# Masked attention on compacted slots: the context's products of two slot blocks run in a row, with nine buffers for exponentials instead of five

## The chip, the cores and the metric

The kernel runs on one core of one Trainium2 chip, as one launch. The metric is the device time of that launch in microseconds; the figure for the kernel before is the median of three runs. Traces come from one further execution that the hardware profiler recorded.

The engines are named as the profile names them: PE is the matrix engine, PEld its weight loads, ACT the engine of the exponentials and of most copies out of PSUM, DVE the vector engine, POOL the engine that issues indirect gathers and scatters, SP the queue that issues all other DMAs.

## The reference, cut to what matters

```python
x = x + _L0_cond_ref(x, cond_2048, L0_cond_Wq, L0_cond_Wo)   # x: 16 x 512 x 1024

B, D, T = x.shape                     # 16, 512, 1024; NH = 8 heads of dk = 64
scale = 1.0 / jnp.sqrt(dk)
xt = jnp.transpose(x, (0, 2, 1))
q = xt @ Wq.T
qh = q.reshape(B, T, NH, dk).transpose(0, 2, 1, 3)
scores = scale * jnp.einsum('bhqd,bhkd->bhqk', qh, qh)
cmask = mask[:, None, None, :]
rmask = mask[:, None, :, None]
logits = (scores * cmask + (1.0 - cmask) * NEG) * rmask
attn = jax.nn.softmax(logits, axis=-1)
ctx = jnp.einsum('bhqk,bhkd->bhqd', attn, qh)
ctx = ctx.transpose(0, 2, 1, 3).reshape(B, T, D)
out = ctx @ Wo.T
return jnp.transpose(out, (0, 2, 1))
```

The mask is 0 or 1, about half of each. Query, key and value are the same tensor. A masked key gets no weight, and a masked query gets the plain mean over all tokens.

## The kernel before, in words

**Compaction.** Per batch only the unmasked tokens take part in the attention. They are gathered (POOL, indirect DMA) into C = 544 slots: four blocks of 128 and a tail of 32. Masked tokens get one projected mean row per batch. A check at the end falls back to a plain version when a batch does not fit; this does not happen here.

**Work per batch** (16 batches, `run`, lines 724 to 912). For each of the four pairs of heads p and each slot block i from 0 to 3, `scores` (line 497) is called once for each of the two heads. It makes four f16 products on PE (line 530: 128 x 128 weights, 272 columns; a high and a low half of q, two column halves) into one of two PSUM buffers `pss`, and ACT writes the exponentials (line 533) into a tile `p` of 128 x 544 f32, from a ring of five. The scores are symmetric, so the tile serves directly as the right operand of the context.

`attend(b, p, i, ps)` (line 538) multiplies the two heads' exponentials of block i by the values: four f32 products (line 546: 128 x 64 weights, 272 columns), two for the upper and two for the lower half of the 128 output rows, summed over i in the one PSUM tile `pav`. The profile counts each of these f32 products as two records, so one block is eight records of L546. `attend(b, p, 4, None)` adds the tail (line 549, four records) and ACT copies `pav` to a tile `c` (line 553). Since there is one `pav`, the first product of the next pair waits for this copy.

The tail's own scores, `scores(b, k, None)`, come twice per batch, once for heads 0 to 3 and once for heads 4 to 7: 16 small products (line 510), an exponential (line 513) into the same ring, a split on DVE (lines 518, 519), and four SP DMAs (lines 523, 524) that fill the one tile `pt` which line 549 reads for two pairs. `recip` (line 557) makes the reciprocal sums and has them broadcast by DMA into `rb`; `norm` (line 590) multiplies `c` by `rb` on DVE and splits it for the output projection.

**What sets the order.** A batch has 18 places in a list `S`: the 16 pairs (p, i), and two places for the tails' scores, inserted at places 2 and 11. At each place `run` first calls what is due in `free` (loads, `recip`, `norm`), then the scores of the two heads, then `fill`, then `now`. `fill` is a share of other work `m`, dealt out by hand-written costs in proportion to the place: of the batch after, the transposes of x (line 358), the query products (line 380, cost 1.37 per call of 12 products) and the value transposes (line 423); of the batch before, the output projection (line 625, cost 2.6 per call of 12 products). In the second half of the places a large fill goes ahead of `now`. For a middle batch the costs dealt to places 0 to 17 are 1.45, 2.17, 1.37, 0.55, 1.37, 2.6, 1.37, 0, 2.6, 0.5, 2.6, 0.7, 1.37, 2.74, 0.55, 1.47, 2.6, 0.7.

`now` holds `attend` of the place before: each block's context runs one place after its scores. `attend(b, p, 4)` of pair p goes between the two heads' scores of block 1 of pair p + 1 (the lists `whole` and `tail`); for the last pair it follows block 3's in the next batch's first place.

The calls' order is a priority, not yet the order on an engine: when the program is built, a scheduler takes for each engine the first instruction that it thinks ready, and the engine then executes that fixed order.

Of the kernel before, what the change touches and what calls it, by code (L numbers as in the profile page):

```python
# [10 lines left out]
F32 = mybir.dt.float32  # L11
# [8 lines left out]
P = 128  # L20
# [10 lines left out]
C = 544  # L31
# [18 lines left out]
class Fast:  # L50
# [446 lines left out]
    def scores(self, b, p, i):  # L497


        nc, s = self.nc, self.st[b]  # L500
        if "z" not in s:
            s["z"] = self.sb([P, H, 4], F32, "z", 2)
            s["zt"] = self.sb([P, 2], F32, "zt", 2)
        if i is None:
            pt = self.ps_s.tile([P, 2, 512], F32, tag="s", name="pss")
            for a in range(2):
                for g in range(2):
                    for r in range(HG):
                        xx, k = s["xx"][2 * p + r // 2], r % 2
                        nc.tensor.matmul(pt[r * CT:(r + 1) * CT, g, :CH], lhsT=xx[:, 2 * k, 512:C],  # L510
                                         rhs=xx[:, 2 * k + a, g * CH:(g + 1) * CH], start=(a == 0), stop=(a == 1))
            t = self.sb([P, C], F32, "p", 5)
            nc.scalar.activation(t.rearrange("p (g c) -> p g c", g=2), pt[:, :, :CH], AF.Exp,  # L513
                                 bias=s["nm"][p][:, HG:], scale=SCALE, accum_out=s["zt"][:, p:p + 1])

            hi = self.sb([P, C], F32R, "c", 3)
            lo = t.bitcast(F32R)
            nc.vector.tensor_copy(hi, t)
            nc.vector.tensor_tensor(lo, t, hi.bitcast(F32), ALU.subtract)
            s["pt"] = self.sb([P, 2, C], F32R, "pt")  # L520
            half = slice(0, DK), slice(DK, P)
            for k in range(2):
                nc.sync.dma_start(out=s["pt"][half[k], k, :].bitcast(F32), in_=hi[half[k]].bitcast(F32))
                nc.sync.dma_start(out=s["pt"][half[1 - k], k, :].bitcast(F32), in_=lo[half[k]].bitcast(F32))
            return None
        xx, k = s["xx"][p // 2], p % 2
        pt = self.ps_s.tile([P, 2, 512], F32, tag="s", name="pss")
        for a in range(2):
            for g in range(2):
                nc.tensor.matmul(pt[:, g, :CH], lhsT=xx[:, 2 * k, i * P:(i + 1) * P],  # L530
                                 rhs=xx[:, 2 * k + a, g * CH:(g + 1) * CH], start=(a == 0), stop=(a == 1))
        t = self.sb([P, C], F32, "p", 5)
        self.exp = [nc.scalar.activation(t.rearrange("p (g c) -> p g c", g=2), pt[:, :, :CH], AF.Exp,  # L533
                                         bias=s["nm"][p // HG][:, p % HG:p % HG + 1], scale=SCALE,
                                         accum_out=s["z"][:, p, i:i + 1]).ins]
        return t
# [187 lines left out]
    def run(self, flag):  # L724
        B = self.B
        L = lambda f, *a: lambda: f(*a)
        S = [(p, i) for p in range(NP) for i in range(4)]
        S.insert(2, (0, None))
        S.insert(11, (1, None))
        N = len(S)  # L730

        def xt(n):
# [68 lines left out]
        begin += [(0, L(self.load, "o", c)) for c in range(DC)]  # L801
        begin += [(0, L(self.range_x, 0, c)) for c in range(DC)] + [(0, L(self.range_w, "q"))]
        groups = [(g, min(h, B)) for g, h in ((2, 4), (4, 8), (8, 12), (12, 16)) if g < B]
        todo, whole, tail = [], [], []
        for b in range(B + 1):
            o, n = b - 1, b + 1
            if b == B:
# [2 lines left out]
            free, early, late = {}, [], []  # L810
# [67 lines left out]
            for st, (p, i) in enumerate(S):  # L878
                for f in free.get(st, []):
                    f()  # L880
                if i is None:
                    self.scores(b, p, None)
                else:
                    ps = [self.scores(b, 2 * p, i)]
                    if tail:
                        tail.pop()()
                    ps.append(self.scores(b, 2 * p + 1, i))
                goal = total * (st + 1) / N
                fill = []
                while pos < len(m) and (done + m[pos][0] / 2 <= goal or st == N - 1):  # L890
                    fill.append(m[pos])
                    done += m[pos][0]
                    pos += 1

                big = st >= 4 and [c >= 1 for c, _ in fill if c > 0.1][:1] == [True]
                fill = [f for _, f in fill]
                now = [] if i is None else todo
                for f in fill + now if big else now + fill:
                    f()
                if i is not None:  # L900
                    todo = [L(self.attend, b, p, i, ps)]
                if whole and i == 0:
                    tail.append(whole.pop())
                if i == 3:
                    (whole if p < 3 else todo).append(L(self.attend, b, p, 4, None))
                    if p < 3:
                        free.setdefault(st + 2, []).append(L(self.recip, b, p))
                        free.setdefault(st + 4, []).append(L(self.norm, b, p))
            self.st.pop(b - 4, None)
        bad = self.const.tile([1, 1], F32, name="bad")  # L910
        self.nc.vector.tensor_reduce(bad, self.ok[0:1, :], AX.X, ALU.add)
# [145 lines left out]
```

## Time and profile before

| | us |
|---|---|
| median of 3 runs (1238.45 to 1245.84) | 1238.76 |
| the profiled execution's own time | 1251.64 |
| its span, first to last instruction | 1249.9 |
| PE busy | 1140.9 |
| DVE busy | 714.8 |
| ACT busy | 693.6 |
| POOL busy | 296.0 |

The mean granted clock of PE in the profiled execution is 0.966. Busy time of PE counts pipelined products with modelled ends, so that the rows of a timeline overlap: what one product costs is read from start to start, not from its duration. In the lists of waits, a row names the waiting engine, its output tile and line, the engine and line that ended the wait, and then the total, the number of times and the longest.

### The profile page before, as it was taken

How to read it: one execution, taken by the hardware profiler on the slowest of the kernel's cores; microseconds unless marked ns; L12 is line 12 of the kernel's file. 1: busy time of each engine (PE TensorE's matmuls, PEld its weight loads, DVE VectorE, ACT ScalarE, POOL GpSimd, SP SyncE). 2: the span in 40 equal slices, each digit the busy share in tenths (PEclk: the TensorE clock that was granted, in tenths of full speed). 3: DMA queues.
4: the chain of work that ended last, by engine and by line, in shares of the span. 5: the costliest groups of instructions: out<-in, count | busy, mean ns of one | idle time of the engine just before them, and what ended most of it. 6: DMA issues, size and time to landing. Idle time of an engine off the chain costs nothing. (4 is left out here: it accounts for less than half of the span.)

```text
span 1249.9 us, 23817 instructions
## 1 busy us (share of the span) xinstructions
PE 1140.9 (91%) x8354; PEld 694.5 (56%) x8354; DVE 714.8 (57%) x2262; ACT 693.6 (55%) x1828; POOL 296.0 (24%) x299
## 2 busy tenths in 40 slices
PE   7889989998998999999898999999989989998787
PEld 6456555555665555556565555555556555655343
DVE  6576556484645648465464746647565564746433
ACT  5757555565665555556564656556456455545341
POOL 3010221222012123221124314121331222122631
PEclk8899999999999999989999999899999989999889
DMA  6645445555345555545456455454645545444631
GB/s 210 166 125 147 141 128 153 157 161 161 89 138 141 167 149 150 159 122 146 134 140 205 133 149 160 126 150 129 205 129 153 140 142 138 110 138 119 211 114 68
DMA packets 106479, 181.36 MB, mean 145 GB/s; under 512 B 28096, under 2 KB 46176, under 8 KB 106352
## 3 DMA queue, kind: packets, MB, share of 16 engines
q1 hardware_dynamic: 85168, 111.59, 33.4%
q0 software_dynamic: 21184, 68.18, 17.1%
q8 instruction: 68, 1.11, 0.4%
q14 instruction: 59, 0.48, 0.1%
HBM read 92.34 MB, written 33.87 MB: 101 GB/s over the span
## 5 line engine op out<-in xcount | busy, mean ns | idle before, releaser
L533 ACT ACTIVATE p<-pss,nm 128x544 f32<-128x544 f32 x512 | 363.8, 714 | 270.2 <-PE pss L530 190.1
L530 PE MATMUL pss<-xx 128*128 128x272 f16 x2048 | 309.7, 284 | 43.9 <-ACT p L533 24.5
L546 PE MATMUL pav<-p,v 128*64 128x272 f32 x2048 | 328.7, 411 | 15.3 <-issue 11.4
L530 PEld LDWEIGHTS <-xx 128*128 128x128 f16 x2048 | 186.1, 99 | 138.6 <-issue 106.2
L694 POOL DMA_INDIRECT y_out<-xa,idx x72 | 76.9, 1068 | 661.0 <-DVE xa L630 633.7
L546 PEld LDWEIGHTS pav<-p,v 128*64 128x64 f32 x2048 | 132.1, 137 | 134.5 <-issue 80.9
L380 PE MATMUL pm<-xh,wqh 128*128 128x274 f16 (+1 forms) x512 | 147.7, 288 | 20.0 <-ACT q L383 19.7
L380 PE MATMUL pm<-xh,wql 128*128 128x274 f16 (+1 forms) x512 | 147.4, 288 | 0.0
L380 PE MATMUL pm<-xl,wqh 128*128 128x274 f16 (+1 forms) x512 | 147.2, 287 | 0.0
L380 PEld LDWEIGHTS <-wqh 128*128 128x128 f16 x1024 | 101.6, 100 | 48.3 <-issue 25.9
L383 ACT ACTIVATE q<-pm 128x272 f32<-128x272 f32 (+1 forms) x128 | 50.9, 398 | 96.8 <-PE pm L380 69.6
L533 ACT ACTIVATION_READ_ACCUMULATOR p<-pss,nm 128x1 f32 x512 | 102.1, 199 | 0.0
L284 POOL DMA_INDIRECT xa<-x_in,idx x72 | 73.1, 1016 | 90.7 <-ACT p L513 52.1
L630 DVE SCALAR_TENSOR_TENSOR xa<-pm,xa 128x512 f32<-128x512 f32 (+1 forms) x61 | 42.1, 689 | 90.5 <-PE pm L625 86.7
L625 PE MATMUL pm<-woh,ch 128*128 128x512 f16 x240 | 92.8, 387 | 0.0
L625 PE MATMUL pm<-wol,ch 128*128 128x512 f16 x240 | 92.4, 385 | 0.0
L625 PE MATMUL pm<-woh,cl 128*128 128x512 f16 x240 | 92.1, 384 | 0.0
L309 ACT ACTIVATE xm<-xm 128x512 f32<-128x512 f32 x116 | 73.0, 630 | 1.6 <-DMA xm<-x_nat_in 1.6
L694 POOL DMA_INDIRECT y_out<-xi,idx x56 | 58.9, 1051 | 62.1 <-DVE r L568 21.7
L625 PEld LDWEIGHTS <-ch 128*128 128x128 f16 x480 | 47.5, 100 | 46.8 <-issue 3.5
L609 DVE TENSOR_TENSOR c<-c,rb 128x544 f32<-128x544 f32 x64 | 46.1, 721 | 43.7 <-DMA rb<-rd 38.6
L319 DVE SCALAR_TENSOR_TENSOR xl<-pm,xh 128x512 f16<-128x512 f32 (+1 forms) x75 | 44.3, 607 | 33.8 <-ACT xh L318 29.3
(194 smaller groups left out, 1550.6 us busy)
## 6 DMA issues: line engine op xcount, KB each, us to landing
xm<-x_nat_in SPq DMA_DIRECT2D x116, 256.0 KB
xx<-hl SPq DMA_DIRECT2D x256, 68.0 KB
xx<-hl SPq DMA_DIRECT2D x128, 136.0 KB
rb<-rd SPq DMA_DIRECT2D x128, 128.0 KB
pt<-c SPq DMA_DIRECT2D x64, 136.0 KB
pt<-p SPq DMA_DIRECT2D x64, 136.0 KB
ub<-ud SPq DMA_DIRECT2D x16, 256.0 KB
xi<-x_nat_in SPq DMA_DIRECT2D x8, 256.0 KB
```

Source lines behind the costliest of these rows:

```text
L284: self.pool = [self.nc.gpsimd.indirect_dma_start(out=tile[:n], out_offset=None, in_=self.x, in_offset=bass.IndirectOffsetOnAxis(ap=idx, ax ...
L309: self.nc.scalar.activation(s["xm"][k], s["xm"][k], AF.Copy, accum_out=s["ms2"][:, k:k + 1])
L319: self.xs = nc.vector.scalar_tensor_tensor(self.xl[dst], src, SX, self.xh[dst], ALU.mult, ALU.subtract).ins
L380: nc.tensor.matmul(pq, lhsT=w[:, c, e * P:(e + 1) * P], rhs=xx[:, c, cols], start=(k == 0), stop=(k == 3 * DC - 1))
L383: nc.scalar.activation(s["q"][:, e, cols], pq, AF.Copy, scale=1.0 / (SX * SW))
L530: nc.tensor.matmul(pt[:, g, :CH], lhsT=xx[:, 2 * k, i * P:(i + 1) * P], rhs=xx[:, 2 * k + a, g * CH:(g + 1) * CH], start=(a == 0), stop=(a ...
L533: self.exp = [nc.scalar.activation(t.rearrange("p (g c) -> p g c", g=2), pt[:, :, :CH], AF.Exp, bias=s["nm"][p // HG][:, p % HG:p % HG + 1 ...
L546: nc.tensor.matmul(s["pav"][k * DK:(k + 1) * DK, g, :CH], lhsT=s["v"][p][:, i, k * DK:(k + 1) * DK], rhs=ps[k][:, cols], start=(i == 0), s ...
L609: nc.vector.tensor_tensor(c, c, s["rb"][p], ALU.mult)
L625: nc.tensor.matmul(po[:cols.stop - cols.start], lhsT=a[:, e, cols], rhs=w[:, e, :], start=(e == 0 and k == 0), stop=(e == DC - 1 and k == 2))
L630: self.nc.vector.scalar_tensor_tensor(x, po, 1.0 / (SX * SW), x, ALU.mult, ALU.add)
L694: i = self.nc.gpsimd.indirect_dma_start(out=self.out, out_offset=bass.IndirectOffsetOnAxis(ap=idx, axis=0), in_=x, in_offset=None).ins
```

## The change

Five edits, all in the order of the work:

- The ring `p` has nine tiles instead of five, in both places where it is allocated.
- A block's `attend` is kept in `todo`. At blocks 0 and 2 of a pair, what stands in `todo` becomes `ready` and nothing of it runs; at blocks 1 and 3 what is `ready` runs as `now`. So blocks 0 and 1 run together at block 3, and blocks 2 and 3 together at block 1 of the next pair (with the tail's product behind them for the last pair of a batch, at the next batch's place 1).
- `attend(b, p, 4)` of pairs 0 to 2 moves from between the scores of the next pair's block 1 to between those of its block 2.
- The second tail's scores move from place 11 to place 13, behind blocks 2 and 3 of pair 2.
- `norm` of pairs 0 to 2 is due five places after block 3 instead of four.

```diff
-            t = self.sb([P, C], F32, "p", 5)
+            t = self.sb([P, C], F32, "p", 9)
...
-        t = self.sb([P, C], F32, "p", 5)
+        t = self.sb([P, C], F32, "p", 9)
...
-        S.insert(11, (1, None))
+        S.insert(13, (1, None))
...
-        todo, whole, tail = [], [], []
+        todo, ready, whole = [], [], []
...
                     ps = [self.scores(b, 2 * p, i)]
-                    if tail:
-                        tail.pop()()
+                    if i == 2 and whole:
+                        whole.pop()()
                     ps.append(self.scores(b, 2 * p + 1, i))
...
-                now = [] if i is None else todo
+
+                now = []
+                if i in (0, 2):
+                    ready, todo = todo, []
+                elif i in (1, 3):
+                    now, ready = ready, []
                 for f in fill + now if big else now + fill:
                     f()
                 if i is not None:
-                    todo = [L(self.attend, b, p, i, ps)]
-                if whole and i == 0:
-                    tail.append(whole.pop())
+                    todo.append(L(self.attend, b, p, i, ps))
                 if i == 3:
                     (whole if p < 3 else todo).append(L(self.attend, b, p, 4, None))
                     if p < 3:
                         free.setdefault(st + 2, []).append(L(self.recip, b, p))
-                        free.setdefault(st + 4, []).append(L(self.norm, b, p))
+                        free.setdefault(st + 5, []).append(L(self.norm, b, p))
```

## The prediction

> **What bounds the kernel now.** I read the page first, for the engines and the costliest groups.
>
> ```profile
> span 1249.9 us, 23817 instructions
> PE 1140.9 (91%) x8354; PEld 694.5 (56%) x8354; DVE 714.8 (57%) x2262; ACT 693.6 (55%) x1828; POOL 296.0 (24%) x299
> ...
> L533 ACT ACTIVATE p<-pss,nm 128x544 f32<-128x544 f32 x512 | 363.8, 714 | 270.2 <-PE pss L530 190.1
> L530 PE MATMUL pss<-xx 128*128 128x272 f16 x2048 | 309.7, 284 | 43.9 <-ACT p L533 24.5
> L546 PE MATMUL pav<-p,v 128*64 128x272 f32 x2048 | 328.7, 411 | 15.3 <-issue 11.4
> ...
> L533 ACT ACTIVATION_READ_ACCUMULATOR p<-pss,nm 128x1 f32 x512 | 102.1, 199 | 0.0
> ```
>
> PE sets the time: it is busy for 91% of the span, every other engine for under 60%, and ACT waits mainly for PE's scores. The context products (L546) are its largest group, and almost nothing waits for their inputs: 15.3 us idle ahead of them in all. So what counts is how PE strings its products together. For that I read PE's timeline of one batch from the middle, from 628.81 us (the first context run after a batch's end) to 702.42 us (the last of the next).
>
> ```profile
> 626.01 1.14 PE L546 MATMUL pav<-p,v 128*64 128x272 f32 x8
> 627.08 0.66 PE L423 MATMUL pm<-ident,q 128*128 128x128 f32 x4
> ...
> 628.81 1.14 PE L546 MATMUL pav<-p,v 128*64 128x272 f32 x8
> ...
> 631.36 1.09 PE L530 MATMUL pss<-xx 128*128 128x272 f16 x8
> 632.38 0.67 PE L546 MATMUL pav<-p,v 128*64 128x272 f32 x2
> 633.30 0.27 PE L574 MATMUL pm<-ident,r 128*8 128x128 f32 x1 [0.25 <-DVE xl L319]
> 633.50 0.68 PE L546 MATMUL pav<-p,v 128*64 128x272 f32 x4
> 634.12 0.66 PE L358 MATMUL pm<-ident,xa 128*128 128x128 f32 x4
> 634.70 0.67 PE L546 MATMUL pav<-p,v 128*64 128x272 f32 x2
> 635.30 0.66 PE L358 MATMUL pm<-ident,xa 128*128 128x128 f32 x4
> ...
> 641.56 1.13 PE L546 MATMUL pav<-p,v 128*64 128x272 f32 x6
> 642.62 0.21 PE L473 MATMUL pm<-ident,m 4*128 4x4 f32 x1
> ...
> 658.84 0.28 PE L380 MATMUL pm<-xl,wqh 128*128 128x274 f16 x1
> 658.96 0.28 PE L380 MATMUL pm<-xh,wql 128*128 128x274 f16 x1
> 659.17 1.14 PE L546 MATMUL pav<-p,v 128*64 128x272 f32 x8
> 660.24 1.10 PE L530 MATMUL pss<-xx 128*128 128x272 f16 x8
> 661.27 1.14 PE L546 MATMUL pav<-p,v 128*64 128x272 f32 x8
> 665.15 1.76 PE L530 MATMUL pss<-xx 128*128 128x272 f16 x8 [2.74 <-ACT p L533]
> 666.70 0.63 PE L625 MATMUL pm<-woh,ch 128*128 128x512 f16 x1
> 667.13 0.63 PE L625 MATMUL pm<-wol,ch 128*128 128x512 f16 x1
> ```
>
> Read from start to start. Two f16 products follow each other by 0.12 us (658.84, 658.96), but from an f16 product to a context run it is 0.21 us (658.96, 659.17): **entering costs 0.09 us**. A run of eight records, one block, takes 1.07 us (626.01 to 627.08), a run of four 0.62 us (633.50 to 634.12): four records more cost only 0.45 us, some 0.23 us for each concurrent pair, so that a run carries about 0.15 us that does not grow with its length. A lone product of two records takes 0.60 us (634.70 to 635.30), as much as two products side by side. Hence **each separate run costs 0.09 + 0.15 = 0.24 us** beyond its steady work, and a product torn from its partner costs nearly twice its share (six records, three products, take 1.06 us from 641.56 to 642.62).
>
> In this batch the timeline has 20 such runs where 16 blocks would need 16: thirteen of eight records, two of six, one of four and four of two, 128 records together. Most of the torn ones lie between 632 and 638 us, among the next batch's transposes (L358).
>
> Last I read the list of waits.
>
> ```profile
> ACT p L533 <- PE pss L530: 190.1, 154, 3.9
> ...
> PE pss L530 <- ACT p L533: 24.5, 13, 4.4
> ...
> PE pm L380 <- ACT q L383: 19.7, 8, 2.9
> ...
> PE pav L546 <- ACT c L553: 3.9, 6, 0.9
> ```
>
> PE's waits are few and go to ACT: for a score buffer (24.5 us), for a query copy (19.7 us), and for the copy that frees `pav` (3.9 us). A long one costs more than itself, as the view by windows shows for the stretch behind the wait of 2.74 us.
>
> ```profile
> core 0: us, PE busy (x) PEld busy (x) DVE busy (x) ACT busy (x) POOL busy (x), PEclk, DMA share, GB/s
> 646.00:652.00 6.00, 6.00 (x42) 3.43 (x38) 3.51 (x15) 3.69 (x11) 0.00 (x0) 1.00 0.59 158
> 665.50:668.50 3.00, 3.00 (x12) 1.38 (x10) 1.41 (x6) 2.90 (x10) 0.79 (x1) 0.50 0.60 175
> ```
>
> The granted clock (PEclk) is 0.50 there, and the output products step by 0.43 us (666.70, 667.13).
>
> **The change part by part.**
>
> *Two blocks in a row.* 256 blocks become 128 pairs. Two runs of eight cost 2 x (1.07 + 0.09) = 2.32 us. One run of sixteen adds four pairs at 0.23 us, 1.07 + 0.09 + 0.92 = 2.08 us. That saves 0.24 us a pair, **128 x 0.24 = 31 us**, all of it on PE's own path. No run of sixteen is in this trace; the seam between two blocks could at worst cost as much as a fresh run (saving 0), at best what the seams within a run do (saving 31). I take the best, since within a run every record already loads its weights afresh (2048 loads in the row below) and the second column half goes to another PSUM bank.
>
> ```profile
> L546 PEld LDWEIGHTS pav<-p,v 128*64 128x64 f32 x2048 | 132.1, 137 | 134.5 <-issue 80.9
> ```
>
> The Trainium skill has the cause: "TensorEngine Tiling (Array Packing)", section Key Properties, says that a change of tiling mode drains the array, while a change of tile does not, and these products use the two 64-column halves. "TensorE: Matmul & The Clock Gate", section "Step-by-step: what each phase is for", puts a drain at about 128 cycles, at full clock 0.05 us; two drains a pair would save an estimated 14 us instead of 31, and the total would be 1227 us, inside the forecast's own range. The rows show more than that for each run.
>
> *Torn runs.* The seven torn runs of the batch hold three blocks and take 4 x 0.60 + 0.62 + 2 x 1.06 = 5.14 us, where three whole runs take 3.21, and four more entries are 0.36: 2.3 us a batch, 37 us if all 16 batches are like this one. They are torn where blocks of pair 0 meet the transposes of places 0 and 1. Now blocks 0 and 1 come at place 4, behind the transposes, but blocks 2 and 3 of the last pair come at place 1, among them. Bounds 0 and 37; I take a third, **12 us**, as only one run in eight stays there but a ready block is also the scheduler's handiest filler elsewhere.
>
> *Uneven places.* The context work of 1.16 us at every place becomes 2.08 us at every second one, and none at the others. At places 3, 7, 9 and 14 the fill is dealt at 0.55, 0, 0.5 and 0.55, and the costs are close to us (12 query products by 0.12 are 1.4 against 1.37). There PE has its eight scores, 1.03 us with the entry behind them (660.24 to 661.27), and some 0.5 us of fill or of the tail's product, 1.5 us in all. ACT needs two exponentials of 714 + 199 ns, 0.91 each; the first begins after half the scores, so the second ends at 0.5 + 1.83 = 2.3 us, while the next block's second score wants that buffer at 1.5 + 0.5 = 2.0 us.
>
> ```profile
> L553 ACT COPY c<-pav 128x544 f32<-128x544 f32 x64 | 38.7, 605 | 21.0 <-remote 7.9 <-PE pss L530 7.4 <-PE pav L549 2.8
> L425 ACT COPY v<-pm 128x512 f32<-128x512 f32 x64 | 37.4, 585 | 37.9 <-PE pm L423 26.3 <-PE pm L440 5.8 <-issue 3.9
> ```
>
> One copy of 0.6 us on ACT in that place makes 0.3 us late into 0.9. Before, the 1.16 us covered it. That is 64 places at 0.3 to 0.9 us, 19 to 58 us, as an upper bound; below it stands 0, since the older pair is ready all the while and can be put there when the order is fixed, and then a run is broken for 0.24 us, 15 us in all. I take **17 us lost**, near the cheap end. What waits behind PE's late score is everything on PE, since its order is fixed.
>
> *The copy of `pav`* now has a whole place and more ahead of the next pair's first product: the 3.9 us go. *Nine tiles* are what the longer lag needs: at block 3's scores eight tiles are alive, with a tail's nine, so no exponential should wait for a context product; if one does, its score buffer comes free late by up to the two blocks' 2.08 us.
>
> *The second tail* moves two places with its 16 products, exponential, two DVE splits and four DMAs.
>
> ```profile
> 598.70 0.65 PE L510 MATMUL pss<-xx 128*32 128x272 f16 x16
> ...
> 602.78 0.72 DVE L519 TENSOR_TENSOR p<-p,c 128x544 fp32r<-128x544 f32 x1
> 603.57 1.16 SPq L524 DMA_DIRECT2D pt<-p  x2
> ...
> 616.51 0.76 PE L549 MATMUL pav<-pt,vt 128*128 128x272 f32 x4
> ```
>
> From its products to the product that reads `pt` are 17.8 us, and from the last DMA's issue 11.8 us. It starts two places later, 8 us at about 4.1 us a place (73.6 us between 628.81 and 702.42, over 18), and its reader comes one place later: some 7.7 us stay for the DMAs. On DVE its 1.2 us go behind the value sums of place 11 and ahead of the split of q at place 13; on SP its four DMAs go ahead of that split's six as before, on POOL four gathers that followed it are now issued ahead, and their transfers share the DMA engines with its own. The split of q is read only by the next batch's scores. Cost 0; without this cover it would be the part of a landing beyond 7.7 us, once a batch. *`norm`* a place later is DVE's work, and DVE is idle for 43%; pair 2's stays in the last place. 0. *At the end* two blocks instead of one follow the last scores: 1.1 us lost at most, and I take 1.
>
> **The sum**, against the profiled execution: -31 - 12 - 4 + 17 + 1 = **-29 us**, from 1251.64 to 1222.6 us. The median of the runs stands 12.9 us below that execution; the terms are stretches of PE, not of the profiler, so I subtract the same 29 from 1238.76: **1210 us**.
>
> **The rivals.**
>
> *Not what it says:* the fixed order tears the pairs again. For it speaks that 20 runs stand for 16 blocks now; against it that both blocks' inputs are old when they come up. With as many runs as now only the 4 us of the copy and the end's 1 remain, 1236 us.
>
> *Starved by ACT, slower:* the four thin places per batch each wait 0.9 us, because the order is fixed by durations that the chip does not keep. For it: the 24.5 us of just this wait, and 55% of ACT in two-exponential bursts. Against it: ACT's own waits for PE are eight times as long. Then the time is 1238.76 + 58 - 31 - 12 - 4 + 1 = 1251 us. It decides from 46 / 64 = 0.7 us a thin place. Half clock would come on top: the stretch from 665.5 us above ran at 0.50. The Trainium skill warns of it in "TensorE: Matmul & The Clock Gate", section "A second HAM failure mode: psum-queue depth-cycling": short idles between groups that cycle through PSUM make the clock fall again and again. The waits here of 0.3 to 0.9 us are shorter than the one that the trace shows it after.
>
> *Better than summed:* all torn runs go, 37 instead of 12 us. For it: the torn blocks are of pair 0, which moves away from the transposes. Then -54 us, 1185 us.
>
> **How the numbers follow.** The forecast has 0.61, its own range 1194 to 1228; not what it says 0.14, starved 0.13, better 0.12. The range reaches from the better case's time to most of the way to the starved one, 1186 to 1244 us. A measurement of this kernel tells about 1% from no change, 12 us: faster by more than that is the better case and nearly all of the forecast, 0.70; within it 0.17 (the second case and the forecast's edge); slower 0.13.
>
> **What would show it.** Right: about ten context runs a batch, most of sixteen records at about 2.0 us; torn runs only at a batch's start; L546's busy time down by 30 to 45 us from 328.7; no wait of L546 for the copy. PE's wait for L533 may grow from 24.5 to some 40 us. The forecast is wrong if runs stay at eight records (second case), if that wait exceeds 70 us or the granted clock falls clearly under 0.966 (starved), or if a run of sixteen takes 2.2 us or more, which would make the seam cost what a run does. A wait of L549 for `pt` would refute the cover of the second tail.

## The result, and the profile after

The changed kernel took 1203.88 us (median of 4 runs, 1197.65 to 1206.33) beside 1242.3 us before: a ratio of 0.9691 (0.965 to 0.9731), 38 us faster. The forecast was 1210 us against 1238.76, a ratio of 0.977. The change was measured twice more: 0.9653 (0.9588 to 0.9717) on a chip where the kernel before takes 1260.29 us, but only **0.9937 (0.9918 to 0.9956) on a chip where it takes 1150.11 us**. I call the chips that need 1240 us or more for the kernel before the slower ones (the first measurement and the first eight experiments), the two that need about 1150 us the quick ones (the last four experiments). So the total was forecast well on the slower chips, and most of it came from something that the forecast had not seen.

The page of the changed kernel, the lines that answer to those of before:

```profile
span 1200.5 us, 23638 instructions
PE 1117.5 (93%) x8354; PEld 705.2 (59%) x8354; DVE 707.1 (59%) x2262; ACT 683.6 (57%) x1828; POOL 297.6 (25%) x299
...
L533 ACT ACTIVATE p<-pss,nm 128x544 f32<-128x544 f32 x512 | 364.3, 716 | 271.5 <-PE pss L530 220.8
L530 PE MATMUL pss<-xx 128*128 128x272 f16 x2048 | 312.3, 283 | 37.0 <-ACT p L513 15.4
L546 PE MATMUL pav<-p,v 128*64 128x272 f32 x2048 | 312.6, 406 | 0.6 <-ACT c L553 0.4
```

The span is 49.4 us shorter (1249.9 to 1200.5). PE's busy time gives 23.4 of it (1140.9 to 1117.5), and only 16.1 is L546 (328.7 to 312.6), where 30 to 45 was forecast. The other 26.0 us are time in which PE did nothing (span less busy: 109.0 before, 83.0 now). The profiled execution of before was one of its slower ones, so the medians differ by 38 us only. PE's own list of waits now:

```profile
PE pss L530 <- ACT p L513: 15.4, 9, 4.3
PE pm L574 <- DVE r L572: 10.8, 14, 0.9
PE pss L530 <- ACT p L533: 10.3, 10, 2.2
...
PE pav L546 <- ACT c L553: 0.4, 1, 0.4
```

The eight waits for the query's copy (19.7 us) are gone, the wait for the exponentials of the blocks has fallen from 24.5 to 10.3 instead of growing to 40, the copy of `pav` delays the context by 0.4 us instead of 3.9, and 11.4 us that stood ahead of the context with no releaser shown are gone, too. Two waits have grown: for the exponential of the tails' scores (L513) from 5.8 to 15.4 us, and for DVE's reciprocals (L572), which were not in the list, to 10.8. The whole list sums to 73 us, against 100 before. The trace's clock records have 18 half-clock stretches before, 88 us in all, and 11 now, 52 us; the view by cores has the mean granted clock:

```profile
core 0: 1200.5 us, clock 0.979
```

The granted clock was 0.966 before. The timeline of PE in the middle of the run, at a batch's end and the next one's start:

```profile
524.21 0.21 PE L473 MATMUL pm<-ident,m 4*128 4x4 f32 x1
524.36 2.05 PE L546 MATMUL pav<-p,v 128*64 128x272 f32 x16
526.34 0.64 PE L530 MATMUL pss<-xx 128*128 128x272 f16 x4
...
535.62 0.62 PE L530 MATMUL pss<-xx 128*128 128x272 f16 x4
536.17 0.67 PE L546 MATMUL pav<-p,v 128*64 128x272 f32 x2
536.77 0.66 PE L358 MATMUL pm<-ident,xa 128*128 128x128 f32 x4
537.27 0.63 PE L530 MATMUL pss<-xx 128*128 128x272 f16 x4
537.82 0.68 PE L546 MATMUL pav<-p,v 128*64 128x272 f32 x4
538.43 0.27 PE L574 MATMUL pm<-ident,r 128*8 128x128 f32 x1
538.64 1.59 PE L546 MATMUL pav<-p,v 128*64 128x272 f32 x10
540.16 0.52 PE L549 MATMUL pav<-pt,vt 128*128 128x272 f32 x2
```

A run of sixteen takes 1.98 us (524.36 to 526.34), as the price of 0.23 us per further pair said: the seam between two blocks costs nothing. But the pair at 536 us is torn into 2, 4 and 10 records, the first two each behind the four score products of one head. PE's program of the changed kernel has 222 context runs, of which 71 are whole pairs; before it had 314, of which 215 were whole blocks. The change needs 128. In the trace, 71 of the change's 151 runs that are not whole pairs stand directly ahead of scores; before, it was 11 of the 99 that were not whole blocks.

### The profile page after: what moved, and what is told of

It reads as the page before. It is cut to its first block, busy times and chain, and to the rows that moved or that the text cites. A ratio compares the mean times of both kernels' runs of the same rounds, so it can differ in the third digit from the quotient of the medians.

```text
span 1200.5 us, 23638 instructions
## 1 busy us (share of the span) xinstructions
PE 1117.5 (93%) x8354; PEld 705.2 (59%) x8354; DVE 707.1 (59%) x2262; ACT 683.6 (57%) x1828; POOL 297.6 (25%) x299
## 5 line engine op out<-in xcount | busy, mean ns | idle before, releaser
L530 PE MATMUL pss<-xx 128*128 128x272 f16 x2048 | 312.3, 283 | 37.0 <-ACT p L513 15.4
L546 PE MATMUL pav<-p,v 128*64 128x272 f32 x2048 | 312.6, 406 | 0.6 <-ACT c L553 0.4
L546 PEld LDWEIGHTS pav<-p,v 128*64 128x64 f32 x2048 | 143.6, 137 | 109.7 <-issue 46.4
L380 PE MATMUL pm<-xh,wqh 128*128 128x274 f16 (+1 forms) x512 | 144.7, 283 | 1.0 <-issue 0.4
L380 PE MATMUL pm<-xl,wqh 128*128 128x274 f16 (+1 forms) x512 | 143.8, 281 | 1.3 <-issue 1.3
L380 PE MATMUL pm<-xh,wql 128*128 128x274 f16 (+1 forms) x512 | 143.7, 281 | 0.0
L380 PEld LDWEIGHTS <-wqh 128*128 128x128 f16 x1024 | 98.9, 98 | 24.7 <-issue 5.7
L694 POOL DMA_INDIRECT y_out<-xi,idx x56 | 62.8, 1121 | 65.6 <-DVE xi L690 24.8
L284 POOL DMA_INDIRECT xi<-x_in,idx x56 | 57.9, 1034 | 17.1 <-issue 17.1
```

Source lines behind the costliest of these rows:

```text
L284: self.pool = [self.nc.gpsimd.indirect_dma_start(out=tile[:n], out_offset=None, in_=self.x, in_offset=bass.IndirectOffsetOnAxis(ap=idx, ax ...
L380: nc.tensor.matmul(pq, lhsT=w[:, c, e * P:(e + 1) * P], rhs=xx[:, c, cols], start=(k == 0), stop=(k == 3 * DC - 1))
L546: nc.tensor.matmul(s["pav"][k * DK:(k + 1) * DK, g, :CH], lhsT=s["v"][p][:, i, k * DK:(k + 1) * DK], rhs=ps[k][:, cols], start=(i == 0), s ...
L694: i = self.nc.gpsimd.indirect_dma_start(out=self.out, out_offset=bass.IndirectOffsetOnAxis(ap=idx, axis=0), in_=x, in_offset=None).ins
```

## The experiments

The kernel before ran beside each experiment on the same chip: at a median of 1256.22 us for the first four, 1260.29 for the next four, 1148.86 for the next three and 1150.11 for the last. Ratios are to it; a ratio from one group beside one from another compares two chips. The numbers of context runs are counted in each kernel's program for PE.

**The ring alone** (the kernel before with nine tiles; the order on every engine is unchanged).

```diff
-            t = self.sb([P, C], F32, "p", 5)
+            t = self.sb([P, C], F32, "p", 9)
```

> The kernel before with nine tiles in the ring p and nothing else; the order of the instructions on every engine is that of before. If the exponentials or products now and then wait for a free tile in the ring of five (a rival to both other causes), the time falls by 10 us or more below the kernel before. My theory (short runs and a short lag are what cost) expects no change within 1%, with L546 busy 329 us and about 100 us of waits listed on PE.

Measured: 1253.01 us, ratio 0.9976 (0.9933 to 1.0019), L546 busy 327.1 us, PE's listed waits 107 us. The ring of five was no bound by itself.

**The lag alone** (the change, but one block per place, two places after its scores).

```diff
-                if i in (0, 2):
-                    ready, todo = todo, []
-                elif i in (1, 3):
-                    now, ready = ready, []
+                if i is not None:
+                    now, ready, todo = ready, todo, []
...
-                self.last(o, todo)
+                self.last(o, ready + todo)
```

> The changed kernel, but with the context of one block at every place, two places after its scores: the long lag without the two blocks in a row. PE's program has 315 context runs, 214 of them of one whole block, as before (314 and 215). The theory that the runs carry the gain (two blocks in a row) expects L546 at 329 us and the time of the kernel before, 1235 to 1245 us. The theory that the lag carries about half of it, since a ready block stands between the scores and the next wait for ACT, expects the listed waits on PE to fall from 100 to about 75 us, the granted clock to rise to 0.98, and 1218 to 1226 us.

Measured: 1227.53 us, ratio 0.9805 (0.9736 to 0.9875). Its page:

```profile
span 1224.0 us, 23629 instructions
...
L546 PE MATMUL pav<-p,v 128*64 128x272 f32 x2048 | 325.4, 409 | 0.6 <-ACT c L553 0.6
```

The head of PE's list of waits:

```profile
PE pm L574 <- DVE r L572: 10.8, 15, 3.2
PE pss L510 <- issue: 10.7, 15, 1.9
PE pss L530 <- ACT p L533: 9.7, 11, 2.4
```

The context products cost what they did before, and yet 2% are gained: PE's listed waits are 79 us, the clock is 0.978, and the waits for the query's copy are not in the list. The theory that the runs alone carry the gain falls. The change itself was not run on this chip; beside the 3.1% and 3.5% that it gained on two slower ones, the lag and what moves with it (the ring, the second tail, `norm`) are worth somewhat over half.

**The row alone** (the kernel before with nine tiles and with pairs, but one place earlier than in the change; everything else as before).

```diff
-                now = [] if i is None else todo
+                now = []
+                if i in (0, 2):
+                    now, todo = todo, []
...
-                    todo = [L(self.attend, b, p, i, ps)]
+                    todo.append(L(self.attend, b, p, i, ps))
```

> Nine tiles and two blocks in a row, but one place earlier than in the change (blocks 0 and 1 at block 2, blocks 2 and 3 at block 0 of the next pair), with everything else where it was before. PE's program has 194 context runs, 99 of them of two whole blocks (the change: 222 and 71). By the prices read before (1.07 us a block, 1.99 us two, 0.60 a lone product, 0.09 an entry) L546 takes 295 us with its entries, against 331 before and 315 in the change. If only the runs count, it is faster than the change: 1242 - 36 = 1206 us less what the change gains elsewhere is not lost, so 1185 to 1200. If the lag counts too, the waits on PE stay near 100 us and the clock near 0.966, and it is 1205 to 1215 us.

Measured: 1212.6 us, ratio 0.9677 (0.9607 to 0.9748).
The page:

```profile
span 1211.7 us, 23652 instructions
...
L546 PE MATMUL pav<-p,v 128*64 128x272 f32 x2048 | 294.2, 404 | 12.2 <-ACT c L553 7.5
```

L546 lands on the 295 us of the prices. The waits, 96 us, and the clock, 0.970, stay near where they were before, and the wait for the copy of `pav` is back (7.5 us). It reaches the change's time by the other half: fewer runs (194) in place of fewer waits.

**Glued pairs** (the change, with the two blocks queued at a higher priority behind the scores of their place, `self.sm`).

```diff
+    def glued(self, blocks):
+        with self.tc.high_priority(offset=HPO), self.behind(self.sm):
+            for f in blocks:
+                f()
...
-                    now, ready = ready, []
+                    now, ready = [L(self.glued, ready)], []
```

> The changed kernel with the two blocks' products bound together: they get a higher priority and queue behind the scores of their place, so that PE's program has 128 context runs, all of two whole blocks. By the prices, L546 takes 266 us with its entries against 315 in the change. If torn runs are pure loss, it is up to 49 us faster than the change, 1155 to 1175 us. If the torn products stand where PE would wait for ACT anyway, the waits on PE grow by as much and the time stays at 1195 to 1210 us.

Measured: 1203.65 us, ratio 0.9586 (0.9522 to 0.965). The context's line on the page (its number has moved with the edit):

```profile
L551 PE MATMUL pav<-p,v 128*64 128x272 f32 x2048 | 266.6, 403 | 0.0
```

The price is met to the microsecond (266), 46 us less than in the change, but PE's listed waits are 102 us instead of 73, and at most about 1% is gained: 0.9586 against 0.9653 and 0.9691 for the change on other chips, intervals that touch. So much of what was torn probably stood where PE would wait.

**The second tail's place alone** (the kernel before).

```diff
-        S.insert(11, (1, None))
+        S.insert(13, (1, None))
```

> The kernel before, with the second tail's scores at place 13 instead of 11 and nothing else; five tiles, each block's context one place after its scores, 318 context runs in PE's program. In before, eight waits of about 3 us for the query's copy (19.7 us listed) lie at place 11, beside these scores, and each is followed by a half-clock stretch. If the tail's place is what the long lag's gain of 2% really comes from, these waits go and the time falls by 12 to 25 us below the kernel before. If the lag is the cause, no change within 1%, with about 100 us of waits listed on PE.

Measured: 1241.98 us, ratio 0.9857 (0.982 to 0.9895). I had put the gain down to the lag; this one line has 1.4% of its own on this chip. The waits for the query's copy, which came some 9 us after these scores had begun, are gone, and the clock is 0.976. (Of the eight waits before, of 1.8 to 2.9 us, five had a half-clock stretch behind them, not each.) The wait for the tail's own exponential (L513) has grown to 10.6 us from 5.8.

**The lag without the tail's move** (the lag alone, with the tail at 11 and two tiles `pt`).

```diff
-        S.insert(13, (1, None))
+        S.insert(11, (1, None))
...
-            s["pt"] = self.sb([P, 2, C], F32R, "pt")
+            pt2 = s.setdefault("pt", {})[p] = self.sb([P, 2, C], F32R, "pt", 2)
...
-                        free.setdefault(st + 5, []).append(L(self.norm, b, p))
+                        free.setdefault(min(st + 5, N - 1), []).append(L(self.norm, b, p))
```

> The run with one block per place, two places after its scores, but with the second tail's scores back at place 11 (and two tiles pt, so that the tail of the first two pairs is still there when it is read). 313 context runs. If the lag is the cause, 1.5 to 2.5% below the kernel before, as with the tail at place 13 (1.95%), with listed waits on PE near 80 us. If the tail's place is the cause, the time of the kernel before, with the eight waits for the query's copy back.

Measured: 1224.51 us, ratio 0.9729 (0.9692 to 0.9766), PE's listed waits 85 us. The lag does it without the tail's move, the tail's move does some of it without the lag, and both together (0.9805, on another chip) are not seen to be better than one. I read this so: on these chips what counts is which of PE's instructions stand behind the moments at which ACT is late. How much each edit takes of that is not settled.

**Chained pairs** (the change; the first product is placed freely, the others of the two blocks queue behind it, `self.head`, at a higher priority).

```diff
+    def chained(self, blocks):
+        self.head = None
+        for f in blocks:
+            f()
+        self.head = False
...
+                    with ExitStack() as st:
+                        if self.head:
+                            st.enter_context(self.tc.high_priority(offset=HPO))
+                            st.enter_context(self.behind(self.head))
+                        one = nc.tensor.matmul(...).ins
+                    if self.head is None:
+                        self.head = one
...
-                    now, ready = ready, []
+                    now, ready = [L(self.chained, ready)], []
```

> The changed kernel with the two blocks' products chained: the first is placed as in the change, the others queue behind it with a higher priority, so that a run is not torn but may start wherever the first product fits. 130 context runs, 127 of two whole blocks. By the prices L546 takes 267 us with its entries, as in the glued kernel. If it was the glued runs' fixed place behind the scores that brought PE's waits back from 73 to 102 us, these fall to 75 to 90 us and the time is 1 to 2% below the glued kernel's ratio of 0.9586, so 0.94 to 0.95. If any whole run of 2 us keeps the next scores from coming in time, the ratio stays at 0.955 to 0.965.

Measured: 1188.71 us, ratio 0.9423 (0.939 to 0.9456), **about 2% below the change** on the same chip (1188.71 against the 1212.07 us of the next run, 1.9%; the ratios are 2.4% apart). Its page has:

```profile
L557 PE MATMUL pav<-p,v 128*64 128x272 f32 x2048 | 269.1, 403 | 2.6 <-issue 1.4
```

PE's listed waits are 96 us: they should have fallen to 75 to 90 from the glued kernel's 102 and did not, though the gain is as expected. Whole runs pay here, against the change. That they pay because the scheduler may choose their start is argued only, as the glued kernel ran on another chip.

**The change again**, on the same chip as the chained pairs.

> The changed kernel itself, unchanged, beside the others on the same chip. All theories expect a ratio of 0.965 to 0.973 to the kernel before, as first measured.

Measured: 1212.07 us, ratio 0.9653 (0.9588 to 0.9717).

**Whole blocks at the old lag** (the kernel before, each block chained as above).

```diff
-                now = [] if i is None else todo
+                now = [] if i is None or not todo else [L(self.chained, todo)]
```

> The kernel before (lag of one place, one block at a time), with each block's four products chained so that no run is torn: PE's program has 259 context runs, 253 of them of one whole block, instead of 314 and 215. By the prices L546 takes 299 us with its entries against 331. If torn runs are loss, it is 25 to 32 us below the kernel before, a ratio of about 0.975 to 0.98. If the torn products only filled places where PE waits, the ratio stays at 0.99 to 1.0.

Measured: 1131.55 us, ratio 0.9867 (0.9835 to 0.9898). L546 is 296.3 us, 32 below the profile of before (of a slower chip), but only 15 us reach the end: between the two expectations. This chip ran the kernel before at 1148.86 us, 7.5% below the first, and PE's listed waits in this kernel are 35 us.

**Single whole blocks at the long lag** (the lag alone, chained).

```diff
-                    now, ready, todo = ready, todo, []
+                    now, ready, todo = [L(self.chained, ready)] if ready else [], todo, []
```

> One block per place, two places after its scores, nine tiles, the second tail at place 13, each block chained: 255 whole runs of one block. Against the chained pairs (130 runs) only the two blocks in a row are missing. By the prices that is 125 runs x 0.25 = 31 us, L546 at 298 instead of 267 us. If these 31 us reach the end, the ratio is 0.025 above that of the chained pairs, about 0.967. If waits eat them, it is 0.945 to 0.955.

Measured: 1127.24 us, ratio 0.982 (0.9793 to 0.9848), L546 291.6 us. Here the lag adds about 0.5% to the whole blocks, by intervals that just overlap.

**The chained pairs again**, on the same chip.

> The chained pairs once more, beside the other two on the same chip. Expected: the ratio 0.9423 (0.939 to 0.9456) again.

Measured: 1107.47 us, ratio 0.9642 (0.9616 to 0.9668), not the expected 0.9423. First the page of this run:

```profile
span 1104.8 us, 23657 instructions
...
PE 1057.5 (96%) x8354; PEld 696.9 (63%) x8354; DVE 704.7 (64%) x2262; ACT 684.7 (62%) x1828; POOL 295.0 (27%) x299
```

The page of the same kernel on the earlier chip:

```profile
span 1192.9 us, 23657 instructions
...
PE 1086.0 (91%) x8354; PEld 704.5 (59%) x8354; DVE 706.9 (59%) x2262; ACT 687.5 (58%) x1828; POOL 291.6 (24%) x299
```

They are 88 us apart, of which 60 us are PE's idle time (span less busy, 47.3 and 106.9); the rest is busy time, at a granted clock of 0.990 here and 0.973 there. Between single and paired whole blocks lie 1127.24 - 1107.47 = 20 us, of 27.5 us that L546 loses (291.6 to 264.1): between the two expectations.

**The change a third time**, to see which kind of chip its gain belongs to.

> The changed kernel once more. Its runs of products are worth 16 us by the prices (L546 315 us with entries against 331); what is beyond that I now put down to waits that come with late signals from PE to ACT, which one of the chips hardly has. If this falls on a chip on which the kernel before takes under 1200 us, the ratio is 0.978 to 0.987 (16 us and about 0.5% for the lag); on one with 1235 us or more it is 0.965 to 0.973 again.

Measured: 1143.62 us, ratio 0.9937 (0.9918 to 0.9956), beside a kernel before of 1150.11 us: a quick chip again, and less than the 0.978 to 0.987 expected of it. The list of ACT's waits on this chip begins:

```profile
ACT p L533 <- PE pss L530: 247.3, 133, 6.0
ACT q L383 <- PE pm L380: 63.3, 79, 2.2
ACT v L425 <- PE pm L423: 31.3, 24, 1.5
```

And the same list in the first profile of the change:

```profile
ACT p L533 <- PE pss L530: 220.8, 135, 5.7
...
ACT q L383 <- remote: 31.4, 13, 3.7
...
ACT p L513 <- remote: 11.7, 3, 6.6
```

"remote" is a signal for which the records give no sender in time. Every profile of the slower chips has such rows; of the four profiles of the quick chips none has one. The rows alone are weak evidence, since the slower chips' traces also hold fewer signals than their instructions give (1216 for the 1295 of PE before, beside 1250 for 1251 in this third run of the change). The instructions' own times, below, do not depend on that.

## Why the prediction was right in its total, and where its steps failed

The direction and the size were right, the way there only in part. The forecast had 43 us off the context's products and 14 us lost by waits and the end. In the profiles the products lose 16 us, PE's idle time 26 and its other busy time 7. The misses have opposite signs, so the near total is partly luck; on the quick chip, where the change gains 6.5 us, the same sum is far too large.

*Two blocks in a row, -31 us.* The price was right: a run of sixteen takes 1.98 us, with its entry of 0.09 nearly the 2.08 of the sum, and the kernels whose runs are whole have L546 at 266.6 and 264 to 269 us. On the quick chip, whole pairs against whole singles were worth 20 us. The step that failed is the count: 71 of 128 pairs are whole, and a batch has nearly fourteen runs instead of ten, so that the change's L546 loses 16 us and not 31 + 12. The Trainium skill's rule in "TensorEngine Tiling (Array Packing)", section Key Properties, that a change of tiling mode drains the array and a change of tile does not, agrees with a cost per run that does not depend on its length; two drains at the figure quoted in the prediction, an estimated 0.11 us, are under half of the 0.24 us that the rows show.

*Torn runs, -12 us.* The sign was wrong. Before, 41 of 256 blocks were torn (215 whole), now 57 of 128 pairs are (71 whole). By the prices, torn runs cost 49 us in the change (315 against the 266 of whole pairs), and 32 before (331 against 299). I had named the reason and not priced it: a ready block is the scheduler's handiest filler. It fills the moments at which a score buffer is not free, at the price of a run; the 71 torn runs ahead of scores fit that.

*Uneven places, +17 us.* Not seen. PE's wait for the blocks' exponentials fell from 24.5 to 10.3 us. The fillers are, as I read it, the cover that I named as the lower bound; their cost stands in the torn runs, so that this term and the one before are one trade, which I split and counted with two signs. The glued kernel, whose pairs cannot serve as fillers, is in line with that: 15.8 us of this wait, and 102 in the list.

*The copy of `pav`, -4 us.* Right: 3.9 to 0.4.

*Ring, second tail, `norm`, 0 us.* The ring alone is 0.9976, right. The second tail was costed as covered. For `pt` it is: no wait of L549 is in the list. But on the slower chips the move is not neutral: alone it gives 1.4%, while PE's wait for the tails' exponential grows (5.8 to 15.4 us in the change). I had asked what its move delays, not what its old place did to the query products behind it.

*The missing term.* I read PE's waits for ACT as waits for busy ACT and took them to stay. The timeline of ACT before shows otherwise:

```profile
603.08 0.62 ACT L309 ACTIVATE xm<-xm 128x512 f32<-128x512 f32 x1
603.60 0.19 ACT L309 ACTIVATION_READ_ACCUMULATOR xm<-xm 128x1 f32 x1
607.49 0.40 ACT L383 ACTIVATE q<-pm 128x272 f32<-128x272 f32 x1 [3.70 <-remote]
607.79 0.40 ACT L447 CAST vt<-tmp 128x256 fp32r<-128x256 f32 x1
```

ACT copies out a query product at 607.49 whose last matmul PE started at 602.70:

```profile
602.70 0.28 PE L380 MATMUL pm<-xh,wql 128*128 128x272 f16 x1
602.91 1.14 PE L546 MATMUL pav<-p,v 128*64 128x272 f32 x8
603.98 1.10 PE L530 MATMUL pss<-xx 128*128 128x272 f16 x8
607.94 0.39 PE L380 MATMUL pm<-xh,wqh 128*128 128x274 f16 x1 [2.86 <-ACT q L383]
```

ACT was idle for 3.70 us with its input long made, and PE then stood 2.86 us. The release came late: the trace's signal records have three signals of PE within 0.2 us, at 607.47, 607.60 and 607.65 us, for products that PE's rows end at 602.98, 604.62 and 605.08. What PE can do meanwhile depends on how much work that needs nothing new from ACT stands next in its order. That is what the longer lag supplies, and what the forecast lacked. In the change this copy is late even more (31.4 us of "remote" in 13 waits, 18.2 in 6 before), yet no wait of PE for it is left: the lateness is covered, not gone. The quick chips bear that out: no such rows there, and 0.6% instead of 3.1%. What the lateness costs by itself is not shown, as no experiment took it away on one chip.

No trace of the kernel before was taken on a quick chip, so where 9 of the 16 us that L546 saves went there rests on an estimate. PE's busy time outside L546 is 789 to 793 us in all four quick profiles. With 790 us and the 328.7 of L546 on the first chip, the kernel before would leave PE some 30 us idle in its 1148 us of span there; the change's profile has 41.9. So PE's idle time would have grown by about what is missing, as if torn products had stood in waits. In the whole blocks at the old lag, too, only half of the saving (15 of 32) reached the end.

Of the rivals, "not what it says" is the nearest to what the quick chips show (1236 us is 0.998), "starved" is refuted on both kinds of chip, and "better than summed" fails as the runs that are not whole rose from 99 to 151.

## What to carry to other kernels

When work is moved so that like stands with like, count the runs in the engine's fixed order before pricing them: the scheduler may use the work as filler, and then the seam's price is multiplied by another number. A wait whose input was ready long before is no matter of throughput; give the engine behind it work that depends on nothing recent, and expect the gain only where such waits occur. A gain of 3% on one chip may be 0.6% on the next, so a kernel is to be compared on more than one, and the version to take here is the chained pairs, ahead of the change on both kinds (0.9423 and 0.9653 on one slower chip; 0.9642 and 0.9937 on two quick ones).

## What the runs showed of the hardware that I had not expected

- The same program takes 1104.8 us of span on one chip and 1192.9 on another, and the kernel before 1149 to 1150 and 1242 to 1260 us. The profiles of the slower chips have waits of ACT that end "remote", up to 10.1 us long, those of the quick ones have none. What makes these signals late was not tried and stays open; whether recording the traces takes part in it does, too.
- Changing between the f16 products of the whole array and the f32 products of its halves costs PE some 0.24 us per run, whatever the run's length (which of the two differences costs it was not tried); between two blocks of f32 products with other weights there is no such cost (1.98 us for sixteen records, 1.07 for eight).
